# Four graph layers on one core: layer 3's x transposed by DRAM and VectorE blocks in place of TensorE, with a new written-out order

## The chip, the core and the metric

One core of a Trainium2 chip runs the whole program as one launch. The metric is device time in microseconds (us). Three runs of the kernel before have a median of 2782.68 us (2781.85 to 2784.01).

## What is computed

32 graphs of 512 nodes with 256 features pass through four layers. Each layer adds its result to x and normalises the rows. All is float32. Cut to what matters:

```python
# layer 0: h = (1+eps)*x + adj@x;  y = relu(h@W1 + b1)@W2 + b2
# layer 1: 4 heads, e = leaky_relu(e_dst + e_src) where adj > 0.5, softmax, out = attn@h + bias
# layer 2: 8 heads, scores = q@k.T/sqrt(32) + log(adj + 1e-6), softmax, out = (attn@v)@Wo.T + bo
# layer 3:
intermediate = jnp.einsum('bsh,hd->bsd', matrix, W)
similarities = jnp.einsum('bsd,btd->bst', intermediate, matrix) * adj
attn = jax.nn.softmax(jnp.where(key_mask, similarities, NEG_INF), axis=-1)
output = jnp.einsum('bst,bth->bsh', attn, matrix)
# after each layer: x = layernorm(x + layer(x))
```

In layer 3 the x that enters is needed twice: with its nodes on the partitions (for the last product and the residual) and with its features on the partitions (for `intermediate` and `similarities`, whose sums run over features). The second form is xT3, the transpose of x3.

## The kernel before

Each graph is cut into 4 chunks of 128 nodes and 2 chunks of 128 features. `graph(g)` (line 595) describes one graph as some 300 named steps. A step names its engine, an assumed duration, the steps it comes after, and the buffers that it takes; a buffer is returned when the last step that reads it is done. The steps that the prediction speaks of are these, by name and line (a number at the end of a name counts chunks or halves):

- `la` (814): four loads of the adjacency into `Ar`, in runs of 128 bytes, for which SP's queue issues the transfers; `at` (873) turns the 32x32 blocks on VectorE, which gives the transposed adjacency AT.
- `h`, `f`, `y`: layer 0's products (hT, h1T, y_ps); `he`, `fe`: ScalarE's copies; `x1`, `st1` (692, 635): residual and statistics.
- layer 1: `xt1` (971), `v1`, `Rt` (1028), then a round trip of R through DRAM (`Rs` 1038, `Rl` 1045), `z` on ScalarE (1097), `zm` on VectorE (1108), `o1` (1130), `as` (sums for the denominator, 1158), `d1` (1168), `dt`, `yt` (1197), `st2`.
- layer 2: `xt2`, `q`, `k`, `v2`; then eight times `s` (scores, 1286, four banks of PSUM), `e` (ScalarE's exponentials, 1299), `m` (VectorE's product with AT, 1308), `n` (1344). The exponentials are summed by accumulating DMAs that POOL issues: `cd` (1319, 1 MB each) adds one chunk into another, three for each half of the heads, and `fd` (1372, 512 KB) folds the partitions; `d2` (1391) then sums on TensorE. `nd`, `rc`, `ne`, `yd` (1427 to 1449, VectorE) turn the sums into factors and scale; `p` (o2p_ps) is the output product, with residual and statistics behind it (692, 635).
- layer 3: `r3` (681) writes the normalised x3; `xt3` (1234) are two steps of four TensorE transposes into PSUM, `xe3` (1238) are ScalarE's two copies to SBUF; together they are `features_first(3, ...)`, called at line 1492. Then `i` (iT_ps), `t` (s), `ta` (1524), `te` (1530), `w` (o_ps<-x,z), `wx` and the last normalisation, and `out` (1581).
- `xd1` to `xd3` (622): biases added to x by accumulating DMAs from POOL's queue.

A product can be run in two ways: in one instruction over the whole array, or (line 344) as four instructions of 32 columns each. TensorE loses time when the next instruction divides the array otherwise than the one before; the steps carry that as `mode`, and many products take either mode.

The order of the work is fixed before the launch. `Plan.order` (line 134) walks all steps of all graphs, at most six graphs open at once, with assumed durations. Of the steps that could begin early enough it takes the one that is due first. A step's due time is its graph's turn times a period, less the work behind it, plus a shift that is written out for each step name in the call at line 1594, with extra shifts for the first and last graphs. The result is one program order for each engine; each engine then runs its instructions in that order and waits where an input is missing. SP's and POOL's queues of DMAs are in order too. Several graphs are in flight: while one is in layer 0, the ones before it are in layers 1 to 3.

`turned` (702) stands in the file before the change, but nothing calls it; nor is `moved` (743) called.

Of the kernel before, what the change touches and what calls it, by code (L numbers as in the profile page):

```python
# [9 lines left out]
F32 = mybir.dt.float32  # L10
# [6 lines left out]
P = 128  # L17
# [31 lines left out]
class Plan:  # L49
# [84 lines left out]
    def order(self, period, ahead, window, stay, rush=(), moves=(), edges=(0, (), 0, ())):  # L134


        room = {b: [(0.0, i) for i in range(n)] for b, n in self.stock.items()}
        engine, mode, out, last = {}, "", [], 0.0
        held = [{} for _ in self.steps]
        ends = [{} for _ in self.steps]  # L140
        waits = [{n: len(s.after) for n, s in steps.items()} for steps in self.steps]
        fwaits = [[len(after) for _, after in frees] for frees in self.frees]
        ready, low, opened = {}, 0, 0
        todo = [len(steps) for steps in self.steps]
        moved = dict.fromkeys((n for steps in self.steps for n in steps), 0.0)
        turn = [max(g - 1, 0) for g in range(len(self.steps))]
        for i, early in enumerate(rush):
            turn[-1 - i] -= early
        for n, far in moves:
            moved[n] += far  # L150
        lead, tail = edges[0], len(self.steps) - edges[2]
        early, late = dict(edges[1]), dict(edges[3])

        def shift(g, name):
            return moved[name] + (early if g <= lead else late if g >= tail else {}).get(name, 0.0)

        def near(low):
            fill, until, between, left, drain = ahead
            return fill if low < until else drain if low >= len(self.steps) - left else between

        def open_to(n):
            nonlocal opened
            while opened < min(n, len(self.steps)):
                for name in self.steps[opened]:
                    if not waits[opened][name]:
                        ready[opened, name] = self.ready(opened, name, ends)
                opened += 1

        open_to(window)
        while low < len(self.steps):  # L170
            found = []
            for (g, name), t in ready.items():
                s = self.steps[g][name]
                t = max(t, engine.get(s.eng, 0.0))
                into = self.EITHER.get(mode, "c32") if s.mode == "any" else s.mode
                change = self.CHANGE[into] if s.eng == "pe" and into != mode else 0.0
                for k, (kind, _, rest) in enumerate(s.take):
                    r, n = room[kind], sum(b[0] == kind for b in s.take[:k])
                    if len(r) <= rest + n:
                        break  # L180
                    t = max(t, r[n][0])
                else:
                    due = turn[g] * period - self.left[g][name] + shift(g, name) + stay * change
                    found.append((t, due, g, name, change))
            if not found:
                return math.inf, out
            first = min(found)[0] + near(low)
            _, t, g, name, change = min((due, t, *f) for t, due, *f in found if t <= first)
            s = self.steps[g][name]
            t += change  # L190
            if s.eng == "pe":
                mode = self.EITHER.get(mode, "c32") if s.mode == "any" else s.mode
            del ready[g, name]
            got = {}
            for kind, key, _ in s.take:
                got[key] = held[g][key] = (kind, room[kind].pop(0)[1])
            if s.eng:
                engine[s.eng] = t + s.us
            end = ends[g][name] = t + s.us
            last = max(last, end)  # L200
            out.append((g, name, mode, got))
            for h, n in s.then:
                waits[h][n] -= 1
                if not waits[h][n] and h < opened:
                    ready[h, n] = self.ready(h, n, ends)
            for k in s.frees:
                fwaits[g][k] -= 1
                if not fwaits[g][k]:
                    key, after = self.frees[g][k]
                    kind, i = held[g].pop(key)  # L210
                    free = max(ends[g][a] + self.HOP.get(self.steps[g][a].eng, 0.0) for a in after)
                    room[kind].append((free, i))
                    room[kind].sort()
            todo[g] -= 1
            while low < len(self.steps) and not todo[low]:
                low += 1
                open_to(low + window)
        return last, out
# [12 lines left out]
def fast_path(  # L231
# [23 lines left out]
    nc = tc.nc  # L255
    B, N, D = x.shape
# [67 lines left out]
    def transfer(name, us, after, queue="q1", land=4.0):  # L324

        @step(f"{name}.q", queue, us, after)
        def _():
            pass  # L330

        @step(name, None, land, (f"{name}.q",))
        def _():
            pass
# [260 lines left out]
    def graph(g):  # L595
        plan.graph()
        slot = plan.slot[-1]
        last = g == B - 1
        t = {"g": g}
# [102 lines left out]
        def turned(n, more, src):  # L702

            @step(f"xw{n}i", "sp", 0.45, row(f"r{n}", NC))
            def _():
                t[f"xd{n}"] = dram.tile([N, D], F32, tag=f"x{n}_dram", name=f"x{n}_dram_{g}")
                nc.sync.dma_start(t[f"xd{n}"].rearrange("(c p) d -> p c d", p=P), t[src][:, :, :D])

            transfer(f"xw{n}", 2.0, (f"xw{n}i",), land=6.0)

            for a in range(4):

                @step(
                    f"xl{n}{a}i", "sp", 0.66, (f"xl{n}{a-1}i",) if a else (f"xw{n}",),
                    take=() if a else (f"C=xL{n}/{2 if n == 1 else 1}",) + more,
                )
                def _(a=a):
                    if a == 0:
                        t[f"xL{n}"] = mid(f"xL{n}", [P, DC, N], f"xL{n}")
                    nc.sync.dma_start(  # L720
                        t[f"xL{n}"][32 * a : 32 * a + 32].rearrange("j d (b i) -> j d b i", i=32),
                        bass.AP(
                            t[f"xd{n}"].tensor, t[f"xd{n}"].offset + 32 * a,
                            [[D, 32], [P, DC], [32 * D, N // 32], [1, 32]],
                        ),
                    )

                transfer(f"xl{n}{a}", 1.0, (f"xl{n}{a}i",), land=5.0)

            for d in range(DC):  # L730

                @step(
                    f"xe{n}{d}", "dve", 0.66, row(f"xl{n}", 4) + prev(f"xe{n}", d),
                    take=() if d else (f"C=xT{n}",),
                )
                def _(d=d):
                    if d == 0:
                        t[f"xT{n}"] = mid(f"xT{n}", [P, DC, N], f"xT{n}")
                    nc.vector.transpose(t[f"xT{n}"][:, d, :], t[f"xL{n}"][:, d, :])

            plan.free(f"xL{n}", row(f"xe{n}", DC))

        def moved(n, more, src, shared):
# [17 lines left out]
            for b in range(4):  # L761

                @step(
                    f"xe{n}{b}", "act" if shared else "dve", 1.35 if shared else 1.3,
                    (row(f"xu{n}", DC) if shared else row(f"r{n}", NC)) + prev(f"xe{n}", b),
                    take=() if b else (f"C=xT{n}",) + more,
                )
                def _(b=b):
                    if b == 0:
                        t[f"xT{n}"] = mid(f"xT{n}", [P, DC, N], f"xT{n}")  # L770
                    to = slice(32 * b, 32 * b + 32)
                    for a in range(4):
                        of = slice(32 * a, 32 * a + 32)
                        out = t[f"xT{n}"][to].rearrange("j d (c a i) -> j d c a i", c=NC, a=4)[:, :, :, a, :]
                        if shared:
                            nc.scalar.copy(
                                out, t[f"xU{n}"][of].rearrange("j d (c b i) -> j d c b i", c=NC, b=4)[:, :, :, b, :]
                            )
                            continue
                        for d in range(DC):  # L780
                            nc.vector.transpose(out[:, d], t[src][of, :, d * P + 32 * b : d * P + 32 * b + 32])
# [710 lines left out]
        features_first(3, ("L3",), src="x3")  # L1492
# [589 lines left out]
```

## Time and profile before

| | |
|---|---|
| median of 3 runs | 2782.68 us |
| profiled execution: device time, and the span of its trace | 2784.18 us, 2782.4 us |
| TensorE busy over the span | 98% |
| VectorE, ScalarE, POOL busy | 76%, 62%, 17% |
| xt3 and xt2 transposes together (L1234) | 512 instructions, 75.0 us busy |
| their copies (L1238) | 128 instructions, 72.3 us, 594 ns each |
| VectorE block transposes of the adjacency (L873) | 124 instructions, 77.9 us, 678 ns each |
| accumulating DMAs of 1 MB (L1319) | 186, median 8.1 us from issue to landing |
| DMA engines: POOL's accumulating queue, SP's queue | 52.2% and 17.9% of 16 engines' time |

Busy times on TensorE are those of pipelined instructions: they overlap, so what a step costs is read from the start of one step to the start of the next. "PEld" is the load of weights, which runs beside. A row of the trace names the source line, the operation and the tiles, output first; "idle before" with an arrow tells what the engine had waited for. A table of stretches gives for each stretch the busy time of every engine and the share of its time that the 16 DMA engines were busy.

### The profile page before, as it was taken

How to read it: one execution, taken by the hardware profiler on the slowest of the kernel's cores; microseconds unless marked ns; L12 is line 12 of the kernel's file. 1: busy time of each engine (PE TensorE's matmuls, PEld its weight loads, DVE VectorE, ACT ScalarE, POOL GpSimd, SP SyncE). 2: the span in 40 equal slices, each digit the busy share in tenths (PEclk: the TensorE clock that was granted, in tenths of full speed). 3: DMA queues.
4: the chain of work that ended last, by engine and by line, in shares of the span. 5: the costliest groups of instructions: out<-in, count | busy, mean ns of one | idle time of the engine just before them, and what ended most of it. 6: DMA issues, size and time to landing. Idle time of an engine off the chain costs nothing.

```text
span 2782.4 us, 64791 instructions
## 1 busy us (share of the span) xinstructions
PE 2739.6 (98%) x27204; PEld 1368.5 (49%) x27204; DVE 2123.4 (76%) x4203; ACT 1738.6 (62%) x3374; POOL 476.5 (17%) x526
## 2 busy tenths in 40 slices
PE   8999999999999999999999999999999998999998
PEld 6545345545454445454455554455554443454434
DVE  3878778877778877778877778877778867468975
ACT  3665766667566667566666565666565655466763
POOL 1121211111122111121111121111221111111110
PEclk9999999999999999999999999999999999999999
DMA  8496787677778676777676777677787776927660
GB/s 165 88 172 128 149 175 134 138 150 141 147 146 159 136 151 137 156 137 163 135 151 138 156 143 157 136 151 142 151 149 150 143 151 118 174 52 154 135 126 25
DMA packets 350146, 390.24 MB, mean 140 GB/s; under 512 B 265036, under 2 KB 304920, under 8 KB 317976
## 3 DMA queue, kind: packets, MB, share of 16 engines
q0 software_dynamic: 45568, 277.89, 52.2%
q1 hardware_dynamic: 303296, 107.86, 17.9%
q8 instruction: 216, 3.54, 0.5%
q14 instruction: 82, 0.67, 0.1%
q10 hardware_dynamic: 984, 0.28, 0.1%
HBM read 141.38 MB, written 17.08 MB: 57 GB/s over the span
## 4 chain that ended last, share of the span: by engine, by line
PE 94%; DVE 2%; ACT 1%; DMA 1%; issue 1%; POOL 0%; ACTq 0%; DVEq 0%; POOLq 0%
PE s L1286 9%; PE o_ps L1344 8%; PE o_ps L1130 7%; PE o_ps L344 7%; PE s L344 7%; PE y_ps L340 7%; PE hT_ps L344 6%; PE v_ps L340 6%; PE h1T_ps L340 5%; PE qT_ps L344 3%; PE kT_ps L344 3%; PE iT_ps L344 3%; PE h1T_ps L344 2%; PE o2p_ps L344 2%; PE xT_t L1234 2%; PE v_ps L344 2%
## 5 line engine op out<-in xcount | busy, mean ns | idle before, releaser
L1308 DVE SCALAR_TENSOR_TENSOR z<-AT,z 128x1024 f32<-128x1024 f32 x512 | 614.2, 1212 | 228.4 <-ACT z L1299 227.9
L1299 ACT ACTIVATE z<-s 128x512 f32<-128x512 f32 x1024 | 550.2, 604 | 198.7 <-PE s L1286 151.1
L1319 POOL DMA_DIRECT2D z<-z x186 | 165.2, 890 | 1357.9 <-PE o_ps L1344 434.8
L681 ACT ACTIVATE x<-x,shift,rstd 128x256 f32<-128x256 f32 x508 | 274.2, 594 | 180.1 <-DVE shift L666 173.2
L1097 ACT ACTIVATE z<-R_bc,nT,S 128x512 f32<-128x512 f32 x512 | 377.2, 810 | 6.2 <-DMA z<-z 3.1
L1108 DVE SCALAR_TENSOR_TENSOR z<-z,T,edge 128x512 f32<-128x512 f32 x512 | 347.5, 744 | 12.0 <-ACT z L1097 11.8
L1286 PE MATMUL s<-qT,kT 32*128 32x512 f32 x2048 | 280.9, 629 | 0.0
L658 POOL TENSOR_TENSOR rstd<-ve,nhalf 128x4 f32<-128x4 f32 (+1 forms) x131 | 164.5, 1257 | 577.0 <-DVE ve L652 566.0
L1344 PE MATMUL o_ps<-z,v 128*32 128x512 f32 x2048 | 257.7, 597 | 1.3 <-DVE z L1308 1.3
L1130 PE MATMUL o_ps<-z,v 128*32 128x512 f32 x2048 | 240.7, 598 | 9.7 <-DVE z L1108 9.7
L1158 DVE TENSOR_TENSOR z<-z 128x512 f32<-128x512 f32 (+1 forms) x256 | 233.6, 950 | 3.9 <-PE o_ps L1130 2.7
L635 DVE BATCH_NORM_STATS2 st<-x 128x6 f32<-128x256 f32 x508 | 211.4, 416 | 10.1
L344 PE MATMUL o_ps<-x,z 128*32 128x257 f32 x3648 | 213.7, 380 | 0.0
L344 PE MATMUL s<-iT,xT 128*32 128x512 f32 x1744 | 196.2, 597 | 0.0
L340 PE MATMUL y_ps<-w_sb,h1T 128*128 128x256 f32 x864 | 191.1, 379 | 0.0
L340 PEld LDWEIGHTS y_ps<-w_sb,h1T 128*128 128x128 f32 x864 | 163.9, 190 | 23.0 <-issue 0.7
L344 PE MATMUL hT_ps<-AT,x 128*32 128x384 f32 (+2 forms) x2496 | 173.5, 379 | 0.0
L1286 PEld LDWEIGHTS s<-qT,kT 32*128 32x128 f32 x2048 | 92.0, 183 | 165.5 <-issue 69.6
L344 PEld LDWEIGHTS o_ps<-x,z 128*32 128x32 f32 x3648 | 117.3, 110 | 106.5 <-issue 34.8
L1530 ACT ACTIVATE z<-z,node_off 128x512 f32<-128x512 f32 x128 | 92.0, 720 | 114.7 <-DVE z L1524 114.7
L340 PE MATMUL h1T_ps<-hT,w_sb 128*128 128x512 f32 x340 | 155.5, 593 | 0.4 <-DVE rd L1190 0.4
L1130 PEld LDWEIGHTS o_ps<-z,v 128*32 128x32 f32 x2048 | 66.1, 110 | 159.1 <-issue 136.0
(187 smaller groups left out, 3893.4 us busy)
## 6 DMA issues: line engine op xcount, KB each, us to landing
z<-z POOLq DMA_DIRECT2D x186, 1024.0 KB, 8.1
x<-biases POOLq DMA_DIRECT2D x96, 512.0 KB, 10.7
R_bc<-R_dram SPq DMA_DIRECT2D x32, 1024.0 KB
Ar<-in_adj_dram SPq DMA_DIRECT2D x124, 256.0 KB
z<-z POOLq DMA_DIRECT2D x62, 512.0 KB, 9.3
x<-in_x_dram SPq DMA_DIRECT2D x32, 512.0 KB
out_dram<-x SPq DMA_DIRECT2D x31, 512.0 KB
xs_row<-xs_dram SPq DMA_DIRECT2D x32, 128.0 KB
```

The lines of the kernel that those rows point to most:

```text
L340: nc.tensor.matmul(out, lhsT, rhs, start=start, stop=stop)
L344: nc.tensor.matmul(out[part], lhsT[:, part], rhs, start=start, stop=stop)
L635: nc.vector.bn_stats(t[f"st{n}"][:, c, :], t["xo" if n == 4 else "x"][:, c, :D])
L681: nc.scalar.activation(t[into][:, c, :D] if into else xn, xn, AF.Identity, bias=t[f"shift{n}"][:, c : c + 1], scale=t[f"rstd{n}"][:, c : c ...
L1097: nc.scalar.activation(t[f"e{h}"][:, c, :], t["Rbc"][:, h, :], AF.Relu, bias=t["nT"][:, h, c : c + 1], scale=t["S"][:, h, c : c + 1],)
L1108: nc.vector.scalar_tensor_tensor(z, z, t["T"][:, h, c : c + 1], t["edge"][:, c, :], op0=ALU.add, op1=ALU.mult)
L1130: nc.tensor.matmul(po[32 * q : 32 * q + 32, :], t["v"][:, c, hp * P + 32 * q : hp * P + 32 * q + 32], t[f"e{2*hp+q//2}"][:, c, :], start=( ...
L1158: nc.vector.tensor_add(z[:, :m, :], z[:, :m, :], z[:, m : 2 * m, :])
L1286: nc.tensor.matmul(pk, t["k"][hs, o, blk(c)], t["q"][hs, o, :], start=True, stop=True)
L1299: nc.scalar.activation(t[f"E{k}"][:, j, :], t[f"ps{k}{j}"], AF.Exp, scale=QSCALE)
L1308: nc.vector.scalar_tensor_tensor(z, t["AT"][:, c, None, :].to_broadcast([P, 2, N]), ADJ_EPS, z, op0=ALU.add, op1=ALU.mult,)
L1344: nc.tensor.matmul(t[f"n{o}"][32 * j : 32 * j + 32, :], t["v2"][:, c, o * P + F2 * j : o * P + F2 * (j + 1)], t[f"E{k}"][:, j, :], start=( ...
```

## The change

- In 27 of the 32 graphs (all but 0, 1, 29, 30 and 31) `features_first(3, ...)` is replaced by `turned(3, ...)`. One DMA writes x3 to DRAM, 4096 bytes for each partition in one run; four DMAs read it back into `xL3`, each of them 32 partitions in 1024 runs of 128 bytes; two VectorE instructions of 128x512 transpose its 32x32 blocks into xT3. SP's queue issues the five DMAs; the reads wait for the write. `turned` itself is altered to that layout.
- All numbers of the order are new: period, shifts for every step name, and shifts for the first and last graphs, now also for single graphs (0 to 3 and the last six), for which `order` gets one more argument.
- `moved`, still not called, is altered too.

```diff
-    def order(self, period, ahead, window, stay, rush=(), moves=(), edges=(0, (), 0, ())):
+    def order(self, period, ahead, window, stay, rush=(), moves=(), edges=(0, (), 0, (), ())):
...
+        own = {g % len(self.steps): dict(far) for g, far in edges[4]}
...
-            return moved[name] + (early if g <= lead else late if g >= tail else {}).get(name, 0.0)
+            some = early if g <= lead else late if g >= tail else {}
+            return moved[name] + some.get(name, 0.0) + own.get(g, {}).get(name, 0.0)
...
+        near = g < 2 or g >= B - 3
...
-                t[f"xd{n}"] = dram.tile([N, D], F32, tag=f"x{n}_dram", name=f"x{n}_dram_{g}")
-                nc.sync.dma_start(t[f"xd{n}"].rearrange("(c p) d -> p c d", p=P), t[src][:, :, :D])
+                t[f"xd{n}"] = dram.tile([P, NC, D], F32, tag=f"x{n}_dram", name=f"x{n}_dram_{g}")
+                nc.sync.dma_start(t[f"xd{n}"], t[src][:, :, :D])
...
-                        t[f"xL{n}"] = mid(f"xL{n}", [P, DC, N], f"xL{n}")
+                        t[f"xL{n}"] = mid(f"xL{n}", [P, NC * DC, P], f"xL{n}")
                     nc.sync.dma_start(
-                        t[f"xL{n}"][32 * a : 32 * a + 32].rearrange("j d (b i) -> j d b i", i=32),
+                        t[f"xL{n}"][32 * a : 32 * a + 32].rearrange("j k (e i) -> j k e i", i=32),
                         bass.AP(
                             t[f"xd{n}"].tensor, t[f"xd{n}"].offset + 32 * a,
-                            [[D, 32], [P, DC], [32 * D, N // 32], [1, 32]],
+                            [[NC * D, 32], [P, NC * DC], [32 * NC * D, 4], [1, 32]],
                         ),
                     )
...
-                    nc.vector.transpose(t[f"xT{n}"][:, d, :], t[f"xL{n}"][:, d, :])
+                    nc.vector.transpose(
+                        t[f"xT{n}"][:, d, :].rearrange("p (c f) -> p c f", c=NC),
+                        t[f"xL{n}"].rearrange("p (c d) f -> p d c f", d=DC)[:, d],
+                    )
...
-        features_first(3, ("L3",), src="x3")
+        if near:
+
+            features_first(3, ("L3",), src="x3")
+
+        else:
+
+            turned(3, ("L3",), "x3")
```

## Prediction

> **What bounds the kernel now.** I read the page first, then the chain of work that ended last, then one repeating stretch engine by engine, and last the two ends. The page's first rows and the chain's long pieces:
>
> ```profile
> PE 2739.6 (98%) x27204; PEld 1368.5 (49%) x27204; DVE 2123.4 (76%) x4203; ACT 1738.6 (62%) x3374; POOL 476.5 (17%) x526
> ```
> ```profile
> 1021.23 6.93 PE hT_ps L344 x160
> 1105.16 6.93 PE hT_ps L344 x160
> 1189.08 6.93 PE hT_ps L344 x160
> ```
> ```profile
> 1105.16:1189.08 83.92, 83.92 (x862) 42.42 (x858) 66.39 (x131) 53.91 (x106) 14.90 (x16) 1.00 0.74 147
> 2280.00:2365.00 85.00, 75.09 (x718) 32.72 (x713) 61.77 (x119) 44.81 (x80) 11.27 (x14) 0.92 0.65 124
> ```
>
> Layer 0 of a graph begins every 83.92 us from 517 to 2196 us, and in such a stretch TensorE is busy for all of it: the list of waits has no entry for TensorE between 440 and 2190 us. So what is taken from TensorE there shortens the span one for one, as long as no new wait opens. VectorE has 17.5 us free in each stretch, ScalarE 30, the DMA engines a quarter. TensorE's idle time, 2782.4 - 2739.6 = 42.8 us, lies at the ends: 15.3 us before 432 us, 14 us from 2196 to 2440 us, 13.5 us in the last 180 us.
>
> **What the change does to TensorE.** The steps that go:
>
> ```profile
> 1157.94 2.00 PE L1286 MATMUL s<-qT,kT 32*128 32x512 f32 x16
> 1159.87 0.66 PE L1234 MATMUL xT_t<-ident,x 128*128 128x128 f32 x4
> 1160.37 1.06 PE L340 MATMUL v_ps<-wg_sb,xT 128*128 128x264 f32 x4
> 1161.26 0.60 PE L1234 MATMUL xT_t<-ident,x 128*128 128x128 f32 x4
> 1161.69 1.50 PE L340 MATMUL v_ps<-wg_sb,xT 128*128 128x264 f32 x6
> ```
>
> From start to start the first four transposes take 0.50 us and the second four 0.43; the first group also pays for entering a new division of the array, so a group is 0.43 and a graph loses 0.87 us. 27 graphs: 23.5 us.
>
> The new order also changes how often TensorE changes its division of the array. I counted both built orders: 15 changes in a repeating block before, 14 after; 548 and 542 over the whole program. A change: two score chunks take 1.93 us here, one alone 1.07 (1167.32 to 1168.39), so a following one is 0.86 and entering is 0.21. From the other side, 83.92 less the same starts without changes (about 81.5) leaves 2.4 us for 15, 0.16 each. I take 0.18: 1.1 us. The other products are the same, whole or in quarters: `f` takes 1.72 us either way in this stretch. Sum: 24.6 us, a block of 82.87 us.
>
> ScalarE loses two copies of 0.59 us per graph. It has 30 us free, so nothing.
>
> **What the change adds elsewhere.** VectorE gets two block transposes of 128x512. The nearest row is that of the adjacency, 678 ns each (0.60 from start to start); the reading in pieces of 128 could cost more, up to the 0.72 of the one that reads PSUM. 1.2 to 1.44 us, I take 1.36: VectorE goes from 66.4 of 83.9 to 67.8 of 82.9. In sum nothing; in place it counts below.
>
> Here a rule speaks against the change. The Trainium skill, "VectorE: DVE Perf Modes", "Rules for kernel authors", gives a 128x128 transpose to TensorE if PSUM will do as its target. Per graph the row has 0.87 us on TensorE, against 1.36 on VectorE and five DMAs. If VectorE were the bound, the rule would be right, and the change would cost 27 x 1.36 = 37 us. The stretch has TensorE with nothing free and VectorE with 17.5 us, so I go by the row.
>
> DMA: 4096 runs of 128 bytes. While only the adjacency's runs of 128 bytes move (1153 to 1154.3 us), 660 packets take 51% of 16 engines, 16 ns each: 4.1 us of all engines. The write of 512 KB at the 278 GB/s that SP's queue moved around 1145 us: 1.9 us. The share goes from 0.74 of 83.92 (62 us) to 68 of 82.9, 0.82. Below full, so nothing in sum.
>
> **Where a wait could open.** The built order of the kernel after is fixed, so I add up what stands between a producer and its consumer on TensorE, by the durations above, and set it against what must happen in that time (lines of before).
>
> (a) x3 to `i`. From the end of `p1` of a graph, TensorE has 39 us of other work before its `i`: three `w` (5.2), two `n` (1.7), hT (6.9), `o1` (7.0), `f` (6.9), `d1` and `yt` (1.9), two `s` (1.7), `y` (6.9), five changes. In that time VectorE runs residual, statistics and, in its order, two `m` and six `zm` before the shift of x3, 10.6 us; ScalarE's four `r3` 2.1; the write lands (R's little one takes 3.9 us from issue to the dependent issue); SP issues four reads. An adjacency load of twice the runs holds SP 3.66 us, so a read 1.83, four 7.3; landing 2.6; two transposes 1.36. About 28.5 us: 10 us to spare. From below it is less; from above, with the longest adjacency issue (9.66 us, halved) and R's longest trip (7.2 us), 44 us, a stall of 5. I go by the median, because SP's queue has nothing of its own beside these reads then. What queues behind: on SP the next adjacency load, `out` and the load of x, needed more than 30 us later; on VectorE, behind the waiting `xe3`, the shift of layer 1's norm and with it `xt2`.
>
> (b) The sums of layer 2 to `d2`. POOL's last three before:
>
> ```profile
> 1136.90 0.92 POOL L1319 DMA_DIRECT2D z<-z  x1 [1.64 <-DVE z L1308]
> ...
> 1144.85 0.92 POOL L1319 DMA_DIRECT2D z<-z  x1 [1.12 <-DMA z<-z]
> ...
> 1153.88 0.87 POOL L1372 DMA_DIRECT2D z<-z  x1 [0.81 <-DMA z<-z]
> ```
>
> They landed 7.4, 8.7 and 5.8 us after issue, so the chain was done at 1159.7 and `d2` ran at 1166.3: 6.6 us to spare, while the adjacency was loading. After, the chain starts with `n6` and TensorE has 27 us of work up to `d2`, against 22.8: 4 us to spare, and the adjacency load should come earlier.
>
> (c) `d2` to `p`. Before, 39 us lay between. After, `d2` is followed by four `n`, two `s` and then `p` of the same graph: 3.44 + 1.71 + three changes = 5.65 us. VectorE must do in it, from start to start in the stretch before, two dT (1.35 us), two reciprocals (0.5), two rdT (1.4), two `yd` (0.75) and two masks of the edges (0.7): 4.7 us, with the way there and back as the kernel's planner assumes it (0.2 and 0.13) 5.05. Only 0.6 us to spare, and two `m` of 1.15 us stand in front of it on VectorE. They belong to score chunks whose TensorE work ended about 10 us earlier, so I count them as done: no wait.
>
> **The sum.** 2782.4 - 24.6 = 2757.8 us of span; the profiled execution's 2784.18 us would be 2759.6. The median of the runs is 1.5 us below that execution, so 2758 us, 0.9% faster. The ends I leave as they are: their TensorE work is the same but for the edit, and an order without times does not tell which of its waits there will be late.
>
> **Rivals.**
> - Idle time at the ends goes. Between 2196 and 2440 us TensorE waits for `zm` (8.5 us) and sums of layer 2 (3.1 us and more) where layer 0 of graphs 27 to 31 begins at distances of 129, 59, 56 and 96 us; in the new order the TensorE work between them is 85, 78, 54 and 79 us, more even. All 14 us saved: 2744. Against: the new order has other late waits there.
> - A small stall in each block, at (a) or (b), about 0.5 us in 27 graphs: 2771. For: DMA at 0.82 on average, and in parts of the stretch already at 1.0. Against: 10 and 4 us to spare.
> - Slower: `p` waits at (c). If the two `m` are still to run when `d2` ends, their 2.3 us less the 0.6 spare put 1.7 us on the path in each of some 20 repeating blocks, against a gain of 1.05 there; outside the blocks seven graphs still gain 6 us. 2782.7 + 13 - 6 = 2790. It decides from 1.65 us of delay on VectorE.
> - It does not do what it says: excluded, the built program has 216 fewer transposes, 27 x 8.
>
> **Chances.** Gain as summed, ends within 10 us: 0.62 (2748 to 2768). Ends better: 0.12 (2738 to 2748). A small stall or worse ends: 0.19 (2768 to 2785). Slower by (c) or the like: 0.07. The measurement can tell some 0.2%, 5.6 us, from no change. Faster by more (below 2777): 0.62 + 0.12 + most of 0.19 = 0.88; within: 0.06; slower: 0.06. Range 2744 to 2776.
>
> **What would show it.** Right: layer 0 of a graph every 82.9 us, no wait of TensorE in the middle, the transposes' row at 296 instead of 512 instructions, DMA share near 0.82, SP's reads issued within 8 us. Wrong: in the list of waits, o2p_ps waiting for VectorE's yT (c), d_ps for a DMA (b), iT_ps for xT (a); or more than 43 us of idle TensorE, at the ends. If block transposes in pieces take over 0.9 us, (c) and (a) grow tighter at once.

## The result and the profile after

The changed kernel takes 2765.36 us (median of 4 runs, 2763.07 to 2767.73) against 2782.26 for the kernel before in the same session: a ratio of 0.9941, 95% interval 0.9925 to 0.9956. It is faster by 0.6%, where 0.9% was forecast. The profiled execution's span went from 2782.4 to 2765.3 us, so 17.1 us came where the sum said 24.6. Line numbers of the kernel after are 2 to 15 higher: the product in quarters is L346, whole products L342, layer 2's and layer 3's transposes L1241, the accumulating sums L1326 and L1379, `d2` L1398. New are L710 (the write of x3), L723 (its reads) and L742 (the block transposes).

The first row of the page, and two stretches (columns: length, then busy us and instructions of TensorE, weight load, VectorE, ScalarE, POOL, then granted clock, DMA share, GB/s):

```profile
PE 2716.7 (98%) x28680; PEld 1317.9 (48%) x28680; DVE 2158.8 (78%) x4257; ACT 1720.4 (62%) x3320; POOL 474.8 (17%) x526
```
```profile
1105.16:1188.12 82.96, 82.96 (x927) 40.49 (x922) 67.83 (x133) 54.42 (x105) 15.71 (x17) 1.00 0.86 161
2359.00:2423.00 64.00, 56.03 (x593) 29.10 (x585) 32.17 (x62) 32.15 (x59) 7.04 (x8) 0.95 0.77 151
```

A repeating block, from the start of one graph's layer 0 to the next one's, is 82.96 us long instead of 83.92 (82.87 forecast) and TensorE still fills it. Layer 0 begins at that distance from graph 8 to graph 26. The rows of the transposes, by line:

```profile
L1241 PE MATMUL xT_t<-ident,x 128*128 128x128 f32 x296 | 40.7, 279 | 0.1
L742 DVE STREAM_TRANSPOSE xT<-xL 128x512 f32<-128x512 f32 x54 | 35.6, 692 | 11.9 <-issue 11.6 <-DMA xL<-x_dram 0.2
```

296 transposes are left of 512, and VectorE pays 692 ns for each of its own: both as forecast. What VectorE waited before them, 11.9 us, is nearly all in one place. TensorE's list of waits (line, what it waited for: us in total, times, longest) shows which:

```profile
PE iT_ps L346 <- DVE xT L742: 8.0, 1, 8.0
PE AT_t L853 <- DMA A<-in_adj_dram: 7.2, 3, 4.5
PE d_ps L1175 <- DVE z L1165: 5.8, 4, 3.1
PE ok_ps L1618 <- DVE okr L1616: 3.3, 1, 3.3
```

The first row is the change's own: once, in the second stretch above, `i` of graph 26 waited 8.0 us for the transposed x3. That stretch is 64 us long with 8 us of TensorE idle. It lies in the drain, the time after 2100 us in which the last graphs run out and the blocks no longer repeat.

**Where 7.5 us of the sum went.** TensorE's busy time fell by 2739.6 - 2716.7 = 22.9 us, 1.7 less than summed. Its idle time rose from 42.8 to 2765.3 - 2716.7 = 48.6, by 5.8. Up to the first repeating block it grew from 15.3 to 15.9 us, and the repeating blocks have none. The other 5.1 lie in the drain, which went from 27.5 to 32.7, and this is a balance of more than one wait. Up to 2440 us the kernel before had 14.0 us there, mostly these two:

```profile
PE o_ps L1130 <- DVE z L1108: 8.5, 2, 4.4
PE d_ps L1391 <- DMA z<-z: 3.1, 1, 3.1
```

The new order has neither of them there. The 8.0 us of `i`, 3.1 us at layer 1's sums (the third row of the list above) and smaller ones stand in their place, 14.1 us in all. After 2440 us the idle time went from 13.5 to 18.6 us, in several short waits, the largest new ones these:

```profile
PE o_ps L1137 <- DVE z L1115: 2.5, 2, 1.5
PE o_ps L1351 <- DVE z L1315: 1.4, 1, 1.4
```

So the new order took the old waits away, as the prediction's first rival had it, and brought others of 5 us more. 1.7 + 5.8 = 7.5.

### The profile page after: what moved, and what is told of

It is laid out like the page before. It is cut to its first block, busy times and chain, and to the rows that moved or that the text cites. A ratio compares the mean times of both kernels' runs of the same rounds, so it can differ in the third digit from the quotient of the medians.

```text
span 2765.3 us, 68089 instructions
## 1 busy us (share of the span) xinstructions
PE 2716.7 (98%) x28680; PEld 1317.9 (48%) x28680; DVE 2158.8 (78%) x4257; ACT 1720.4 (62%) x3320; POOL 474.8 (17%) x526
## 4 chain that ended last, share of the span: by engine, by line
PE 86%; DVE 6%; DMA 3%; issue 2%; ACT 1%; POOL 0%; SPq 0%; DVEq 0%; POOLq 0%; ACTq 0%
PE s L1293 8%; PE o_ps L1351 7%; PE v_ps L346 7%; PE y_ps L342 7%; PE o_ps L346 6%; PE o_ps L1137 6%; PE hT_ps L346 6%; PE s L346 5%; PE h1T_ps L346 4%; PE o2p_ps L346 3%; PE iT_ps L342 3%; PE s L342 3%; PE h1T_ps L342 3%; PE kT_ps L342 2%; DVE z L1115 2%; PE qT_ps L346 2%
## 5 line engine op out<-in xcount | busy, mean ns | idle before, releaser
L1306 ACT ACTIVATE z<-s 128x512 f32<-128x512 f32 x1024 | 541.4, 608 | 109.2 <-PE s L1293 103.4
L1326 POOL DMA_DIRECT2D z<-z x186 | 174.4, 942 | 868.4 <-PE o_ps L1351 445.3
L1351 PE MATMUL o_ps<-z,v 128*32 128x512 f32 x2048 | 254.9, 599 | 2.6 <-DVE z L1315 1.4
L1539 DVE TENSOR_TENSOR z<-s,AT 128x512 f32<-128x512 f32 x128 | 88.4, 690 | 214.9 <-PE s L342 110.1
L1137 PE MATMUL o_ps<-z,v 128*32 128x512 f32 x2048 | 233.8, 595 | 2.5 <-DVE z L1115 2.5
L1165 DVE TENSOR_TENSOR z<-z 128x1024 f32<-128x1024 f32 (+1 forms) x256 | 229.5, 949 | 0.7 <-PE o_ps L1137 0.7
L346 PE MATMUL o_ps<-x,z 128*32 128x257 f32 x3520 | 202.4, 380 | 0.0
L346 PE MATMUL hT_ps<-AT,x 128*32 128x256 f32 (+2 forms) x2640 | 185.5, 380 | 0.0
L342 PE MATMUL y_ps<-w_sb,h1T 128*128 128x256 f32 x832 | 184.4, 379 | 0.0
L342 PEld LDWEIGHTS y_ps<-w_sb,h1T 128*128 128x128 f32 x832 | 156.1, 190 | 21.5 <-issue 1.0
L346 PEld LDWEIGHTS o_ps<-x,z 128*32 128x32 f32 x3520 | 114.8, 110 | 83.8 <-issue 6.9
L346 PE MATMUL h1T_ps<-hT,w_sb 128*32 128x512 f32 x1296 | 147.9, 595 | 0.0
L625 POOL DMA_DIRECT2D x<-biases x96 | 103.8, 1081 | 237.0 <-issue 67.7
L346 PE MATMUL s<-iT,xT 128*32 128x512 f32 x1232 | 139.4, 592 | 0.1
```

Source lines behind the costliest of these rows:

```text
L342: nc.tensor.matmul(out, lhsT, rhs, start=start, stop=stop)
L346: nc.tensor.matmul(out[part], lhsT[:, part], rhs, start=start, stop=stop)
L1137: nc.tensor.matmul(po[32 * q : 32 * q + 32, :], t["v"][:, c, hp * P + 32 * q : hp * P + 32 * q + 32], t[f"e{2*hp+q//2}"][:, c, :], start=( ...
L1165: nc.vector.tensor_add(z[:, :m, :], z[:, :m, :], z[:, m : 2 * m, :])
L1306: nc.scalar.activation(t[f"E{k}"][:, j, :], t[f"ps{k}{j}"], AF.Exp, scale=QSCALE)
L1351: nc.tensor.matmul(t[f"n{o}"][32 * j : 32 * j + 32, :], t["v2"][:, c, o * P + F2 * j : o * P + F2 * (j + 1)], t[f"E{k}"][:, j, :], start=( ...
```

## The trip of x3, in the middle and in the drain

The timeline of the kernel after, SP's queue and the consumers only, in a repeating block (start, us, engine, line, operation):

```profile
1114.40 0.57 SPq L710 DMA_DIRECT2D x_dram<-x  x1
1127.76 3.12 SPq L723 DMA_DIRECT2D xL<-x_dram  x4
1131.05 6.58 SPq L821 DMA_DIRECT2D Ar<-in_adj_dram  x4
1136.35 1.30 DVE L742 STREAM_TRANSPOSE xT<-xL 128x512 f32<-128x512 f32 x2
1137.88 3.60 PE L342 MATMUL iT_ps<-xT,w_sb 128*128 128x512 f32 x8
```

The write took 1127.76 - 1114.40 = 13.4 us until the reads could be issued; the prediction's step (a) had 3.9. The four reads held SP 3.12 us, where I had 7.3. From `p1`'s end at 1098.9 the whole way is: 15.5 us to the write's issue (12.7 in the prediction), 13.4 for the write (3.9), 3.1 for the issues (7.3), 5.5 to the first transpose (2.6) and 1.3 for the transposes (1.4). That makes 38.8 us; in the prediction these parts were 27.9, taken as about 28.5. The cover, TensorE's other work in that time, is 39.0 us, so the trip fits by 0.2 us and not by 10.

The block transposes began without a wait, so their start is set by VectorE's order, not by the landing. In graphs 4 to 22 they come 19.8 to 22.1 us after the write's issue, whether the write takes 4.1 us or 14.1. Of the 8.6 us from the first read's issue to the transposes a part is VectorE's order: in graph 17 6.0 us were enough.

The same in the drain, for graph 26:

```profile
2358.33 0.56 SPq L710 DMA_DIRECT2D x_dram<-x  x1
...
2361.70 8.18 SPq L723 DMA_DIRECT2D xL<-x_dram  x4
...
2386.10 1.31 DVE L742 STREAM_TRANSPOSE xT<-xL 128x512 f32<-128x512 f32 x2 [11.56 <-issue]
...
2386.96 1.93 PE L346 MATMUL iT_ps<-xT,w_sb 128*32 128x512 f32 x8 [7.96 <-DVE xT L742]
```

Here the write is quick (3.4 us) and the reads are slow: 2386.10 - 2361.70 = 24.4 us from first issue to use. And there is less beside them. Graph 26's `p1` ended at 2350.8 and TensorE was free for its `i` at 2386.96 - 7.96 = 2379.0, 28.2 us of cover; in the repeating block it is 39.0 us (`p1` ended at 1098.9). From `p1`'s end to the end of the block transposes both take about the same, 36.6 and 38.8 us; what differs is the cover. The DMA part of the page, cut to 2380 to 2384 us, says what filled the engines (queue: packets, MB, share of 16 engines; q0 is POOL's, q1 SP's):

```profile
q0 software_dynamic: 106, 0.86, 103.2%
q1 hardware_dynamic: 8, 0.00, 0.3%
```

POOL's accumulating sums had the engines, 106 packets of about 8 KB, while the last packets of the reads, on which all of x3 hung, hardly moved. The write meets the same in the middle: SP had moved 494 packets from its issue to 1120 us, but from 1120 to 1125.5 us 26, while POOL moved 136, at 97.9% of the engines.

## Experiments

Each kernel was timed beside the kernel before, whose median was 2780.3 to 2781.0 us in these three sessions. None leaves out part of the computation.

**The gain: eight transposes put back.** In the changed kernel, into the bank that `i` takes anyway; their result is overwritten, the trip stays.

```diff
                 pq = t[f"pi{o}"] = bank(f"i{o}", [P, N], f"iT_ps_{o}")
+                if not near:
+                    for c in range(NC):
+                        nc.tensor.transpose(pq[:, blk(c)], t["x3"][:, c, blk(o)], ident)
```

> The kernel after, its order untouched, with the eight transposes of the 27 graphs put back on TensorE as dead work (into the bank of `i`, overwritten by its products). If the gain is TensorE's own time (my theory): 0.87 us more in each of 27 graphs, blocks of 83.8 us, 2765 + 23.5 = 2789 us. If the gain comes from the new order and the transposes were hidden anyway (rival): under 5 us more, blocks near 83.

Measured: 2787.57 us (ratio 1.0026, 1.0014 to 1.0037).

```profile
1105.16:1189.01 83.85, 83.85 (x934) 41.26 (x930) 67.83 (x133) 53.39 (x104) 15.06 (x16) 1.00 0.80 155
```

The block grows from 82.96 to 83.85: eight transposes are 0.89 us (0.87 in the sum). What is left of the gain, 83.92 - 83.85 = 0.07 us, goes to the new order and one change of division fewer, where the sum had 0.18. So nearly all of the middle's gain, 0.89 of 0.96 us, is TensorE time of the transposes. Over the whole program this kernel is 6.9 us slower than the kernel before. So with the transposes' time paid again, the new order and the trip together do not gain but cost; the two traced executions, with spans 1.9 us apart, show only a part of that.

**The trip without the new order.** Before's planning with its own numbers, and the trip in the 27 graphs.

```diff
-        features_first(3, ("L3",), src="x3")
+        if near:
+            features_first(3, ("L3",), src="x3")
+        else:
+            turned(3, ("L3",), "x3")
```

> The kernel before with its own period and shifts, and only the 27 graphs' transposition moved to DRAM and VectorE (the new steps have no shifts of their own). Theory that TensorE's time is all: blocks of about 82.9 us without waits, and ends as before, 2782 - 24 = 2758 us or a little above. Rival, the new order is needed to make room for the trip through DRAM: waits for xT or for VectorE open in each block, 1 us or more, so 2782 us or above.

Measured: 3311.21 us (ratio 1.1908, 1.1892 to 1.1924): this expectation failed by 550 us. Blocks are 101 to 105 us. The new steps had no shift in that call, their neighbours some 250. SP's queue had waited up to 85 us at the write, so I took that for the cause and gave them a shift:

```diff
-... (('R', 88.748), ...
+... (('xw3i', 250.0), ('xw3', 250.0), ('xl30i', 250.0), ..., ('R', 88.748), ...
```

> The planner's call of before (its period and shifts), with the trip through DRAM for 27 graphs, and for the new steps alone a shift of 250, near that of r3 and xe3 in it, where the earlier try had 0 and took 3311. Theory, what that try paid was the new steps' place: SP's write and reads stood ahead of their data and held SP's queue 85 us; at a place like their neighbours' most of it goes, so under 2900. Rival, any trip without an order annealed for it costs as much, because SP's queue of loads stands behind the wait for the write wherever it is put: over 3100.

Measured: 3323.93 us (ratio 1.1953, 1.1937 to 1.1968), blocks again 101 to 105 us. That cause is refuted too. TensorE's list of waits:

```profile
PE hT_ps L344 <- issue: 83.7, 21, 4.0
PE xT_t L1238 <- ACT x L682: 70.7, 92, 6.9
PE o_ps L1134 <- DVE z L1112: 33.5, 13, 8.2
PE o_ps L1348 <- DVE z L1312: 20.6, 28, 2.5
PE iT_ps L344 <- DVE xT L740: 18.8, 22, 7.9
```

`i`, the trip's consumer, waits 18.8 us for x3 of the 540 lost; the larger waits are in layers 0, 1 and 2, whose steps I had not touched, and TensorE's busy time rose to 3000 us at a granted clock of 0.95. Other steps shift every later choice of the planner, so these two runs do not price the trip. They show that the numbers of before, with the new steps at 0 or at 250, did not fit the changed set of steps; other places for the new steps were not tried. What in those two orders makes the busy time longer stays open.

**The drain: graph 26 by TensorE.** The changed kernel with its order, but graph 26's write, reads and block transposes left out, and eight transposes and two copies put at its `i`.

```diff
+LATE = 26
...
+                if g == LATE:
+                    return
...
+                for d in range(DC if g == LATE and o == 0 else 0):
+                    for c in range(NC):
+                        nc.tensor.transpose(pq[:, blk(c)], t["x3"][:, c, blk(d)], ident)
+                    nc.scalar.copy(t["xT3"][:, d, :], pq)
```

> The kernel after, order untouched, but graph 26 alone turned by TensorE and ScalarE right before its `i` (in the bank of `i`); its five DMAs and two block transposes are left out. In the kernel after `i` of graph 26 waits 8.0 us for xT. Theory that this wait is on the path that sets the end: 8.0 us go, 0.9 us of transposes and about 1.5 us of waiting for the two copies come, so 5 to 6 us less, 2760 us. Rival, another late step takes its place (d_ps waits 3.1 us just behind): less than 2 us.

Measured: 2757.93 us (2755.8 to 2767.58; ratio 0.9916, 0.9902 to 0.9930). A second time, beside the changed kernel on one chip:

> The changed kernel itself, beside the three others on one chip. Theory and rivals agree: a ratio of 0.994 to the kernel before, 2763 to 2768 us.

> The changed kernel with graph 26 alone turned by TensorE again (its write, its four reads and its block transposes left out, every other instruction in its place). Theory, the trip of graph 26 lies bare in the drain: it is under the changed kernel by the 8.0 us of wait less the 2 us that the eight transposes cost, so by 4 to 8 us, about 2759. Rival, the drain's idle time is set by what comes after (z, okr, the last sums), so that the same time is waited for elsewhere: within 2 us of the changed kernel.

Measured: the changed kernel 2763.08 us (2762.12 to 2768.3; ratio 0.9939, 0.9926 to 0.9953), this one 2760.5 us (2756.05 to 2766.53; ratio 0.9938, 0.9924 to 0.9952). In its trace the wait is gone, and the stretch from layer 0 of graph 29 to that of graph 30 is 6.5 us shorter (first the changed kernel, then this one):

```profile
2359.65:2424.18 64.53, 56.74 (x590) 29.32 (x585) 32.03 (x62) 32.18 (x59) 7.04 (x8) 0.92 0.76 150
2356.58:2414.64 58.06, 56.70 (x597) 29.72 (x592) 30.87 (x60) 33.36 (x61) 7.10 (x8) 1.00 0.80 151
```

So the wait is the trip's, and taking it away gave 6.5 us there in this execution. In device time it is less sure: both medians are lower than those of the changed kernel, but the intervals overlap. Seven of the ten executions lie below the lowest of the changed kernel's nine (2762.12 us), the other three at 2765 to 2768. The one traced in the first session is the longest of them (2767.58 us): it had no such wait at `i` either, but others in the drain, `d2` for the sums 3.9 us the longest, and its stretch took 64.1 us. So the rival, that another step waits instead, holds in some executions. This kernel has the lowest medians here, by 3 us in the session with both, and that lead is not certain.

**What is spare at (c), `d2` to `p`.** One of the two transposes of d repeated; then both, with `range(2)` in the loop.

```diff
-                nc.vector.transpose(t[f"dT{o}"], t[f"d{o}"])
+                for _ in range(1 + (o == 0)):
+                    nc.vector.transpose(t[f"dT{o}"], t[f"d{o}"])
```

> The changed kernel with one of the two transposes of d repeated in every graph: 0.6 us more of VectorE between d2 and p. My prediction's step (c), 0.6 us to spare there: the extra just fits, at most 0.1 us a block, so 2765 to 2769. Rival, nothing to spare because VectorE's row of steps behind it carries the delay to the next block as well: 0.6 us in each of some 20 blocks, 2777.

> Both transposes of d repeated: 1.2 us more of VectorE between d2 and p. My prediction's step (c): 0.6 us fit, 0.6 are waited for in each of the 20 to 26 blocks, so 12 to 17 us, 2777 to 2782. Rival with nothing to spare: 1.2 us in each block, 2790 to 2796. Rival with far more to spare than the sum showed: 2766.

Measured: 2771.5 us (2766.51 to 2775.95) and 2783.2 us (2781.4 to 2787.14), against 2763.08 in the same session. In the traces a block stays at 82.97 with one and goes to 83.26 with both: of 1.2 us extra, 0.29 lands on the path, so some 0.9 us is spare at that place (0.6 in the prediction). The changed kernel's timeline has the same figure:

```profile
1170.13 1.09 PE L1398 MATMUL d_ps<-z,ones 64*32 64x512 f32 x16
1171.15 3.64 PE L1351 MATMUL o_ps<-z,v 128*32 128x512 f32 x32
...
1174.72 2.00 PE L1293 MATMUL s<-qT,kT 32*128 32x512 f32 x16
1175.37 1.10 DVE L1456 TENSOR_TENSOR yT<-yT,rdT 128x256 f32<-128x256 f32 x3
1176.65 1.93 PE L346 MATMUL o2p_ps<-woT,yT 128*32 128x256 f32 x32
```

TensorE has 6.5 us between `d2` and `p`, and the second `yd` that `p` needs ends at about 1175.8. The expectation for nd_plus1 (2765 to 2769) is missed by 2.5 us. That for nd_plus2 (2777 to 2782) is missed by 1.2 us, and the sum behind it did not come: the middle grew by 6.0 us instead of 12 to 17, start and drain by 13. Of nd_plus1's 8.4 us the traced execution shows only 1.7, and 0.3 of that in the 19 repeating blocks; where the other executions had the rest no trace shows.

**What is spare at (a), the block transposes done twice.**

```diff
+                    for _ in range(2):
                         nc.vector.transpose(
```

> The kernel after, order untouched, with each of the two block transposes of x3 done twice (the same data again). In the kernel after they end at 1137.65 us and `i` begins at 1137.88. Theory that VectorE is tight in this place although it has 15 us free in a block: 1.3 us more less 0.2 of room, about 1.1 us in each block, 2765 + 27 = 2792 us, with iT_ps waiting for xT in the list of waits. Rival, free time in the block takes it up: 2765 to 2768 us.

Measured: 2782.25 us (2779.08 to 2785.59; ratio 1.0007, 0.9999 to 1.0016), blocks of 83.53, +0.57 for 1.4 us of extra work.

```profile
1138.79 2.80 DVE L743 STREAM_TRANSPOSE xT<-xL 128x512 f32<-128x512 f32 x4
1140.39 1.10 PE L342 MATMUL iT_ps<-xT,w_sb 128*128 128x512 f32 x2
1141.64 2.84 PE L342 MATMUL iT_ps<-xT,w_sb 128*128 128x512 f32 x6 [0.15 <-DVE shift L669]
```

I had expected most of it to count. But `i` needs only the first chunk of features to begin: it starts at 1140.39, before the last two of the four transposes are through. So 0.8 us was spare, and of my 10 us for the whole path less than one is left at its end.

**DMA as the next limit: each read twice.** The second copy goes to a scratch in DRAM and nothing reads it.

```diff
+                    nc.sync.dma_start(
+                        t["xag"][32 * a : 32 * a + 32].rearrange("j k (e i) -> j k e i", i=32),
+                        bass.AP(
+                            t[f"xd{n}"].tensor, t[f"xd{n}"].offset + 32 * a,
+                            [[NC * D, 32], [P, NC * DC], [32 * NC * D, 4], [1, 32]],
+                        ),
+                    )
```

> The changed kernel in which each of the four reads is followed on SP's queue by a second one of the same 4096 packets' worth from DRAM to a scratch of DRAM that nothing uses: the change's own transfer load a second time, 27 graphs long, and four more issues of 0.7 us on SP. Theory, DMA has room in the middle (share 0.86 of a block) and the landing at i has about 3 us to spare: blocks stay at 82.97 to 83.1, so 2765 to 2770. Rival, the transfers are by now as much a bound as TensorE, so that doubled reads delay those of A or the accumulating sums: a block grows by 1 us or more, 2785 and over.

Measured: 2779.56 us (2774.91 to 2792.41; ratio 1.0002, 0.9994 to 1.0011), between both expectations: about 15 us above the changed kernel. It is not an even toll. Nine of the 19 blocks of the middle stay at 82.96 to 83.0; the others are 83.1 to 84.8. The waits and one long block (1449.5 to 1533.5 us, 83.99 long) tell which:

```profile
PE iT_ps L342 <- DVE xT L751: 5.0, 6, 1.8
```
```profile
1502.55 1.02 PE L342 MATMUL qT_ps<-xT,wqT 128*128 128x512 f32 x2
...
1503.51 2.12 PE L1407 MATMUL d_ps<-z,ones 64*32 64x512 f32 x16
...
1505.56 2.78 PE L1360 MATMUL o_ps<-z,v 128*32 128x512 f32 x24
```

Six times in the middle `i` waits for the transposed x3, at (a), and graph 26's wait in the drain grew to 9.5 us. The copies also stand between the reads on SP's queue, so a part of this may be the later issue; the run does not tell the two apart. In the block shown `d2` takes 2.12 us instead of 1.09: it begins and then stands for 1.0 us. Its second product needs the sums of the other half of the heads, whose fold POOL had issued at 1494.31, so this is (b), though no row names the fold. The wait stands inside a row, and the block is still counted busy to the last 0.01 us; only starts laid beside a quiet block's show it. So in the changed kernel the transfers still fit, and with each read doubled they no longer do.

## Why the forecast was right in kind and too large by 7 us

- *TensorE bounds the middle, so its removed work counts one for one*: right. Blocks are 82.96 us, and putting the transposes back brings 83.85.
- *Eight transposes, 0.87 us*: 0.89. *Changes of division, 0.18 each*: mis-sized; all that is left beside the transposes is 0.07 us a block. For the whole program, the run with the transposes put back has TensorE busy for 2739.2 us. So the transposes are 22.5 us (23.5 in the sum) and the rest 0.4 (1.1 in the sum), which makes the 1.7; the changed kernel's two traces differ by 0.7 us themselves.
- *ScalarE's copies free, VectorE's 1.36 us free in sum*: right; the block transposes measured 1.3 us a graph and VectorE has 15 us of a block left. The Trainium skill, "VectorE: DVE Perf Modes", "Rules for kernel authors", keeps a 128x128 transpose on TensorE where PSUM will do; with VectorE as the bound that would have been right, by the prediction's 37 us. Here TensorE was the bound, and the measured time is 17 us less.
- *DMA share 0.82*: 0.86 to 0.88 of a block.
- *(a) 10 us to spare*: the size failed, 0.2 us were left. The write's 3.9 us, taken from R's 8 KB, was 13.4 for 512 KB behind POOL's packets; the reads' issue of 7.3 was 3.1, and the other parts took 5.7 more. That no wait opened in the middle does not confirm the sum; as far as this sum goes, that the trip fits is luck.
- *(b) 4 us to spare*: no wait in the middle of the changed kernel, but the size failed here too; doubled reads open a wait of 1.0 us. POOL's three sums, from the timeline of the kernel after:

```profile
1143.68 0.91 POOL L1326 DMA_DIRECT2D z<-z  x1 [7.57 <-PE o_ps L1351]
...
1151.31 0.91 POOL L1326 DMA_DIRECT2D z<-z  x1 [4.67 <-DMA z<-z]
...
1159.72 0.82 POOL L1379 DMA_DIRECT2D z<-z  x1 [2.58 <-DMA z<-z]
```

  From the first issue to `d2` at 1170.13 are 26.5 us, where the prediction had 27. The last of the three landed 8.8 us after its issue (5.8 before the change), at 1168.5, so 1.6 us are spare, and 0.4 to 3.2 us in the repeating blocks.
- *(c) 0.6 us to spare*: about 0.9. The rival that put its slower case there did not come.
- **The failed step: "The ends I leave as they are."** Their idle time grew by 5.8 us. The largest new piece is the 8.0 us of `i`. The graphs that keep TensorE's way are 0, 1 and 29 to 31, but the blocks stop repeating after 2100 us, and graph 26's `i` has 28.2 us of cover where a repeating block has 39.0. I had counted (a) in the repeating block alone. My own sum of the trip, 28.5 us, set against 28.2 would have shown the place, though not the 8.0 us. Graph 26 put back on TensorE shows that wait gone. The rest of the balance, the old waits that went and the short new ones after 2440 us, comes with the new order; no run here takes it apart.

The measured 2765.36 us lies in the case "gain as summed, ends within 10 us". Of the rivals, that of the ends came half true: the old waits went and other ones came.

## What to carry to other kernels

Work moved off the bounding engine paid its own time here and no more, and what carries it elsewhere needs cover in every copy, the last ones too: take the cover of a round trip from the stretch where the loop runs out, not only from the block that repeats. Price a transfer by what shares its engines at that moment, not by a small one on the same queue. The planner's numbers of before did not carry over to other steps; to try an edit alone in such a kernel, keep the order and add or replace work in place, as the runs with dead, doubled and late work did here.

## What was not expected of the hardware

- **Small packets stood behind large ones.** In the drain SP moved 8 packets in 4 us and POOL 106. The Trainium skill, "DMA: Bandwidth & Descriptors", "Queues, rings and completion order", has each engine take turns between the queues, packet by packet. 8 against 106 does not look like even turns, unless SP's last packets lay on few engines or a turn takes more than one of the trace's packets; the trace shows neither, so that stays open. What counts for a sum is the 24.4 us for a read that takes at most 8.6 in the block shown.
- **A run of 4096 bytes did not move as one.** While the write was under way, 1114.40 to 1127.76 us, the DMA part of the page counts 568 - 56 = 512 packets of 512 bytes to 2 KB, so of 1024 each:

```profile
DMA packets 887, 2.62 MB, mean 196 GB/s; under 512 B 56, under 2 KB 568, under 8 KB 695
```

x3's chunks stand apart in SBUF (`[:, :, :D]` of a wider tile), so the run is whole on the DRAM side only. A packed x3 was not tried.
- **A stall can lie inside a busy row.** The 2.12 us of `d2` above counts as busy.
- **The granted clock was lower in stretches where TensorE had waited:** 0.95 and 0.92 in the stretch of graph 26's wait (its two traces) and 1.00 in the same stretch without it, 0.95 over the whole of both runs with before's planning. It is no rule: the first 432 us of the changed kernel have 15.3 us of idle TensorE at 1.00.
